# Second FFNs of a macaron block: g^T from turned experts and turned sums, instead of turning g

## The chip, the cores and the metric

The kernel runs on one core of a Trainium2 chip. Five engines work side by side: TensorE (PE, with its weight loads shown as PEld), VectorE (DVE), ScalarE (ACT), GpSimd (POOL) and SyncE (SP), which here issues every DMA. The metric is the device time of one execution in microseconds (us); the time before is the median of three runs.

## The reference, cut to what matters

The input x has shape (2, 2048, 1024), everything in float32. Three residual steps follow one another, each on a layer norm of x:

```python
x = x + 0.5 * ffn(layernorm(x), A, B, W, bias)      # "first FFN"
x = x + ssm(layernorm(x), ...)                      # state-space scan over time
x = x + 0.5 * ffn(layernorm(x), A, B, W, bias)      # "second FFN", the same weights

def ffn(x, A, B, W, bias):                          # a = 64 experts, r = 16
    vecs = einsum('arh,bsh->bsar', A, x)
    arrows = norm(vecs, axis=-1)
    routes = one_hot(top_k(arrows, 4)).sum(-2) / 4  # per row: 4 of 64 experts
    v = einsum('bsa,bsar->bsr', routes, vecs)       # 16 sums per row
    delta = einsum('bsa,ajr,bsr->bsj', routes, B, v)
    return einsum('bsh,jh->bsj', x, W) + bias + delta
```

Call g the array with `g[s, r, a] = routes[s, a] * v[s, r]`, 16 x 64 = 1024 columns for a row. Then `delta = g @ B`, a product over 1024, just as `x @ W` is.

## The kernel before

**Tiles.** The 4096 rows are cut into 16 chunks of 256 rows (8 per batch element), and a chunk into two blocks of 128 rows. `ffn(kind, c, i)` (L592) adds the work of one block of chunk c: kind "f" is the first FFN, "g" the second; 64 blocks in all. `prepare(c)` (L722) normalises a chunk's rows, turns them to u, projects them and computes the step sizes; `scans(c)` (L863) runs the scan of a chunk over 256 time steps.

**One FFN block.** Three products with [128 x 1024] operands: x with A (into the pair of PSUM banks `pv`), x with W and g with B (both accumulated into the pair `po`). Each is 16 float32 matmuls of 128x512; `products` (L575) issues them as tasks of four. A matmul needs its left operand turned, contraction on the partitions. x^T (`xnt`) comes from DRAM for kind "f" (the host laid it out); for kind "g" it is turned on PE: the scan's result y lies turned in DRAM, is fetched as `yt`, turned back on PE (`back`, L384), added to x1 by DVE (`summed`), and the sum is turned again (`turn`, L553). Between the A product and g stand: `square` (ACT, L631), `choose` (DVE, L641: norms, top 4, routes; its last step writes the routes into the tile `choice`), `routed` (DVE, L658), `total` (DVE, L668: the 16 sums, also into `choice`), `spread` (POOL, L676: g as a product of two broadcasts). Then `turn` makes g^T: eight 128x128 transposes on PE into two banks, two copies by ACT into `gt`. After the B products `close` (DVE, L694) scales and adds the result to x.

**Buffers.** Five PSUM banks serve everything of this kind. A block's `pv` and `po` pairs and the scan's sums are only taken if one bank stays free. There is one buffer each for `g`, `gt` and `yt`, two for `xnt`, `xg` and `choice`, four for `rep` (the scan's broadcast input), sixteen for `h`.

**Scan.** For each of four pairs of 128 channels of a chunk, sixteen units run ACT `decay` (two exponentials of 128x256), DVE `entry` (a product) and two DVE `scan` instructions, ACT `keep` (the state) and POOL `leave` (a product) and `join` (a sum). PE `total` (L973) then sums over states. SP fetches `rep` with a broadcast, two DMAs a unit pair.

**Order.** Nothing is left to a compiler: `Plan` (L77) collects tasks with an engine, a cost, the keys they read and write, the buffers they take and give, and a rank. `order()` (L126) plays them through: at each moment an idle engine takes the ready task of lowest rank whose buffers are free; a task becomes ready on another engine `HOP` after what it needs has ended, a DMA `land` after its issue. The resulting list is emitted as it is, so each engine's instructions stand in that fixed order, and so do SP's DMAs. Costs, landings and ranks are numbers in the code. The W and B products of a block have ranks near -1000, so that they go before nearly everything else on PE; the A products have the block's number n (0 to 63) in the sequence `f_seq`, where first FFNs run three chunks ahead of second ones.

**Start.** `load_all` (L408) loads the weights and takes their column means out of A and W (layer norm's mean): POOL sums the pieces of W (`gather`, L445), PE makes the means (`mean`, L472), DVE subtracts them (`center`, L481). Until then the first block's A product is corrected on PE (`correct`, L461).

Of the kernel before, what the change touches and what calls it, by code (L numbers as in the profile page):

```python
# [36 lines left out]
P = 128  # L37
# [3 lines left out]
TOPK = 4  # L41
# [35 lines left out]
class Plan:  # L77
# [3 lines left out]
    HOP = 0.14  # L81
# [145 lines left out]
def macaron_kernel(  # L227
# [55 lines left out]
    places("choice", 2, [P, NA + len(PADS) + RANK])  # L283
# [7 lines left out]

    plan.pool("x1_d", [dram.tile([P, D], FP, name=f"x1_d{j}") for j in range(2 * NT * 4)])
# [52 lines left out]
    def load_rows(c, i):  # L345
# [16 lines left out]
        if c == 0:  # L362
            add("SP", 0.4, load_t, [], [(xt, 0), (xt, 1)], rank=-74.6 * n - 1008.5 if n else -2000.0,
                take=[xt], land=2.3)
            add("SP", 0.4, load, [], row(x_p), rank=81.1 * n - 1006.8, take=[x_p], land=1.9)
        else:
            add("SP", 0.8, emit, [], [(x_p, q) for q in range(KC)] + [(xt, 0), (xt, 1)],
                rank=n - (1006.5 if c == 1 else 100.0), take=[x_p, xt], land=4.9)

    def load_sum(c, i, rank):  # L370
# [4 lines left out]
        for g in range(2):  # L375
# [8 lines left out]
            def back(g=g, pt=pt, yt=yt):  # L384
# [7 lines left out]
                [(yt, 0)] + ([] if g else row(x_p)), rank=200.9 + rank,  # L392
                take=[yt] if g else [x_p, yt], give=[y_d, x1_d], land=4.3)
# [5 lines left out]
            add("PE", 0.55, back, [(yt, 0)] + row(x_p, g), [(pt, 0)], rank=-38.4 + rank, take=[pt], give=[yt])  # L399
            add("DVE", 0.71, summed, [(pt, 0)] + row(x_p, g), row(x_p, g), rank=-60.6 + rank,  # L400
# [7 lines left out]
    def load_all():  # L408
        def one(dst, src, key, us, rank):
            keys = [(*key, h) for h in range(2)] if isinstance(key, tuple) else [key]  # L410
            add("SP", us, lambda: nc.sync.dma_start(out=dst, in_=src), [], keys, rank=rank, land=3.2)
# [11 lines left out]
        add("POOL", 0.23, lambda: nc.gpsimd.memset(mean_w.tile, 1.0 / D), [], [(mean_w, 0)],  # L423
# [15 lines left out]
        add("PE", 1.3, mean_x, [(xnt, 0), (xnt, 1), (mean_w, 0)], [(pm, 0)], rank=-1200.0, take=[pm],  # L439
            give=[mean_w])  # L440
        add("ACT", 0.36, minus, [(pm, 0)], [(less_m, 0)], rank=-1200.0, take=[less_m], give=[pm])
        for w_sb, name, key in ((wa, "wa", "pv"), (ww, "ww", "po")):
# [9 lines left out]
            for h in range(2 if name == "wa" else 0):  # L452
# [14 lines left out]
                add("PE", 0.47, correct, [(total, 0), (less_m, 0)], [(start[key][h], 0)], rank=-1400.0,  # L467
                    give=[total, less_m])
            for h in range(2):
# [8 lines left out]
                add("PE", 0.59, mean, [(total, 0), (mean_w, 0)], [(pt, 0)], rank=-1000.0, take=[pt],  # L478
                    give=[total, mean_w])
                for k in range(KC):  # L480
# [4 lines left out]
                    add("DVE", 0.55, center, [(pt, 0)], [(name, k, h)], rank=-900.0, give=[pt])  # L485
# [5 lines left out]
        add("POOL", 2.53, lambda: nc.gpsimd.tensor_scalar_mul(half_bias, half_bias, 0.5),  # L491
            [], ["half_bias"], rank=232.4)
# [7 lines left out]
        add("ACT", 0.31, exp_a, [], ["a_neg"], rank=87.5)  # L500
        add("DVE", 0.24, neg_a, [], ["a_neg"], rank=69.0)
# [6 lines left out]
    def spread_of(x_p, st, factor, rank, after=()):  # L508
# [28 lines left out]
        add("DVE", 1.95, stats, row(x_p) + list(after), [(st, 0)], rank=-70.5 + rank, take=[st])  # L537
        add("ACT", 2.63, root, [(st, 0)], [(st, 1)], rank=97.4 + rank)

    def normalize(x_p, xn_p, rank, after=()):  # L540
# [9 lines left out]
        add("ACT", 1.63, scale, row(x_p) + [(st, 1)], [(xn_p, 0), (xn_p, 1)], rank=-24.1 + rank,  # L550
            take=[xn_p], give=[st, x_p])

    def turn(src, keys, dst, out_keys, rank, take=(), give_src=None):  # L553

        for g in range(2):
# [9 lines left out]
            def act(g=g, pt=pt):  # L565
# [3 lines left out]
                rank=-40.0 + rank, take=[pt] + (list(take) if g == 0 else []),  # L569
                give=[src] if give_src else [])  # L570
            add("ACT", 0.58, act, [(pt, 0)], out_keys(g), rank=-141.8 + rank, give=[pt])
# [20 lines left out]
    def ffn(kind, c, i):  # L592
# [21 lines left out]
        for h in range(2):  # L614
# [4 lines left out]
            add("POOL", 1.19, bias, row(x_p, h) + ["half_bias"], row(x_p, h), rank=rank, port=True)  # L619
# [7 lines left out]
        for h in range(2):  # L627
# [10 lines left out]
            add("ACT", 1.02, square, [(pv[h], 0)], [(g_p, h)], rank=-67.7 + rank,  # L638
                take=[g_p] if h == 0 else [])

        def choose():  # L641
# [3 lines left out]
            routes = ch.tile[:, : NA + len(PADS)]  # L645
# [7 lines left out]
            nc.vector.tensor_scalar(routes, routes, CHOSEN, 1.0 / TOPK, ALU.is_equal, ALU.mult)  # L653

        add("DVE", 2.39, choose, [(g_p, 0), (g_p, 1)], [(ch, 0)], rank=-11.4 + rank,
            take=[ch, mk], give=[mk])
        for h in range(2):
# [7 lines left out]
            add("DVE", 0.62, routed, [(pv[h], 0), (ch, 0)], [(g_p, h)], rank=-234.6 + rank,  # L665
                give=[pv[h]])

        def total():  # L668
            nc.vector.tensor_reduce(  # L669
                ch.tile[:, NA + len(PADS) :],  # L670
                g_p.tile.rearrange("p (r a) -> p r a", a=na), AX.X, ALU.add,
            )

        add("DVE", 1.21, total, [(g_p, 0), (g_p, 1)], [(ch, 1)], rank=-13.0 + rank)
        for h in range(2):
            def spread(h=h):  # L676
                v0 = NA + len(PADS) + h * r2
                nc.gpsimd.tensor_mul(  # L678
                    g_p.tile[:, h * HD : (h + 1) * HD].rearrange("p (r a) -> p r a", a=na),
                    ch.tile[:, :NA].unsqueeze(1).to_broadcast([P, r2, NA]),  # L680
                    ch.tile[:, v0 : v0 + r2].unsqueeze(2).to_broadcast([P, r2, NA]),
                )

            add("POOL", 0.99, spread, [(ch, 0), (ch, 1)], [(g_p, h)], rank=-18.0 + rank, port=True,
                give=[ch])
        turn(g_p, lambda g: [(g_p, g)], lambda g: gt.tile[:, g * HC : (g + 1) * HC, :],
             lambda g: [(gt, g)], rank, take=[gt], give_src=True)
# [3 lines left out]
        for h in range(2):  # L691
            products(turn_of, po, h, gt, wb, "wb", False, True, lambda: turn_of.number - 1000.0, [], [gt])

            def close(h=h):  # L694
# [7 lines left out]
                rank=-140.5 + rank, give=[po[h], st])  # L702
# [377 lines left out]
```

## Time and profile before

| what | us |
|---|---|
| median of three runs | 3133.61 (3132.05 to 3138.01) |
| the profiled execution | 3132.46 |
| its span, first to last instruction | 3130.3 |
| PE busy | 3080.1 (98%) |
| DVE busy | 2811.7 (90%) |
| POOL busy | 2280.5 (73%) |
| ACT busy | 1866.3 (60%) |
| granted clock of TensorE, mean | 0.998 |

| group (line, what) | count | busy us | mean ns |
|---|---|---|---|
| L579 A, W and B products, 128x512 | 6144 | 907.4, 891.0, 894.1 | 593 to 595 |
| L561 transposes of g, 128x128 | 512 | 71.7 | 276 |
| L566 ACT copy to gt, 128x512 | 128 | 70.5 | 592 |
| L678 POOL spread, 128x512 | 128 | 139.2 | 1108 |
| L933 DVE scan, 128x256 | 2048 | 1407.7 | 731 |
| L918 ACT decay, 128x256 | 2048 | 974.0 | 478 |

A float32 matmul stands in the trace as two instructions, so 1024 matmuls of each FFN product appear as 2048. Matmuls overlap, so the mean of one is longer than the distance between two starts. A line of waits reads: engine, instruction that waited, "<-" what released it: total us, times, longest.

### The profile page before, as it was taken

What the parts mean: (1) busy time and instruction counts of PE and PEld (TensorE: products, weight loads), DVE (VectorE), ACT (ScalarE), POOL (GpSimd) and SP (SyncE); (2) the same over time, 40 slices, a digit from 0 to 9 for tenths busy, and PEclk for the clock granted to TensorE, in tenths of its full rate; (3) what the DMA queues carried; (4) which work ended last, traced back from release to release, by engine and by line L of the source; (5) the groups of instructions that cost most, each with busy time, mean ns of one, the idle gap of its engine ahead of it and who ended that gap; (6) DMA issues with size and microseconds to landing.
All of it is one profiled execution on the core that took longest, in us unless ns stands there. A gap on an engine that the chain in (4) does not pass through costs nothing.

```text
span 3130.3 us, 36399 instructions
## 1 busy us (share of the span) xinstructions
PE 3080.1 (98%) x9276; PEld 1433.7 (46%) x9276; DVE 2811.7 (90%) x4683; ACT 1866.3 (60%) x4851; POOL 2280.5 (73%) x1818
## 2 busy tenths in 40 slices
PE   7999999999999999999999999999999999999999
PEld 3444444444444444444444444444444444444444
DVE  5279999999999999999989999999999999999951
ACT  2266666666766666767666666666665655555531
POOL 3148787777788877787767777777888788888840
PEclk9999999999999999999999999999999999999999
DMA  6155644655455554554644655456454554555520
GB/s 231 54 162 153 188 142 140 192 153 174 153 164 164 161 177 149 163 173 144 181 148 135 190 153 169 148 156 183 141 171 142 161 162 138 155 161 149 149 73 15
DMA packets 306994, 478.69 MB, mean 153 GB/s; under 512 B 27360, under 2 KB 151904, under 8 KB 306784
## 3 DMA queue, kind: packets, MB, share of 16 engines
q1 hardware_dynamic: 306784, 476.36, 50.3%
q8 instruction: 74, 1.21, 0.2%
q14 instruction: 136, 1.11, 0.1%
HBM read 375.07 MB, written 101.19 MB: 152 GB/s over the span
## 4 chain that ended last, share of the span: by engine, by line
PE 60%; DVE 12%; issue 3%; ACT 2%; DMA 2%; POOL 1%; SPq 0%; DVEq 0%; POOLq 0%; ACTq 0%
PE bank L579 53%; DVE h L933 5%; PE bank L975 3%; DVE h L926 2%; PE bank L561 2%; PE bank L749 1%; PE bank L798 1%; PE bank L386 1%; ACT da L918 1%; DMA xf<-in_x 1%; DVE stats L513 1%; DVE g L659 1%; DVE norms L646 1%; DMA yt<-y_d 0%; DVE choice L653 0%
## 5 line engine op out<-in xcount | busy, mean ns | idle before, releaser
L946 POOL TENSOR_TENSOR h<-h,c 128x512 f32<-128x512 f32 x1024 | 1322.2, 1300 | 419.4 <-ACT state L943 397.9
L933 DVE TENSOR_TENSOR_SCAN h<-da,state,h 128x256 f32<-128x256 f32 x2048 | 1407.7, 731 | 14.1 <-ACT da L918 11.8
L918 ACT ACTIVATE da<-rep,a_neg 128x256 f32<-128x256 f32 x2048 | 974.0, 478 | 673.8 <-DVE h L933 637.2
L579 PE MATMUL bank<-wa,xnt 128*128 128x512 f32 x2048 | 907.4, 595 | 1.4 <-ACT xnt L566 1.4
L579 PE MATMUL bank<-wb,gt 128*128 128x512 f32 x2048 | 894.1, 594 | 6.3 <-ACT gt L566 6.2
L579 PE MATMUL bank<-ww,xnt 128*128 128x512 f32 x2048 | 891.0, 593 | 2.3 <-DVE ww L483 2.3
L965 POOL TENSOR_TENSOR h<-h,h 128x512 f32<-128x512 f32 x512 | 651.4, 1272 | 40.1
L926 DVE TENSOR_TENSOR h<-rep,b 128x512 f32<-128x512 f32 x1024 | 671.6, 665 | 1.4 <-ACT b L880 0.9
L579 PEld LDWEIGHTS bank<-ww,xnt 128*128 128x128 f32 x2048 | 389.7, 190 | 494.1 <-issue 482.7
L579 PEld LDWEIGHTS bank<-wb,gt 128*128 128x128 f32 x2048 | 384.1, 190 | 476.8 <-issue 455.5
L579 PEld LDWEIGHTS bank<-wa,xnt 128*128 128x128 f32 x2048 | 380.5, 190 | 454.1 <-issue 444.1
L678 POOL TENSOR_TENSOR g<-choice 128x512 f32<-128x512 f32 x128 | 139.2, 1108 | 228.7 <-DVE choice L669 228.6
L943 ACT COPY state<-h 128x2 f32<-128x2 f32 x1024 | 188.3, 185 | 55.4 <-DVE h L933 54.3
L632 ACT ACTIVATE g<-bank 128x512 f32<-128x512 f32 x128 | 133.8, 1046 | 74.5 <-PE bank L579 54.5
L533 ACT ACTIVATE stats<-stats 128x1 f32<-128x1 f32 x288 | 58.3, 202 | 139.4 <-DVE stats L528 133.2
L513 DVE BATCH_NORM_STATS2 stats<-xf 128x6 f32<-128x512 f32 x128 | 81.6, 678 | 60.4 <-DMA xf<-in_x 60.4
L617 POOL TENSOR_TENSOR xf<-xf,half_bias 128x512 f32<-128x512 f32 x64 | 83.8, 1329 | 59.3 <-DVE stats L513 59.2
L617 POOL TENSOR_TENSOR xg<-xg,half_bias 128x512 f32<-128x512 f32 x64 | 81.8, 1286 | 60.1 <-PE bank L561 36.9
L975 PE MATMUL bank<-h,summer 128*32 128x512 f32 x1024 | 123.1, 598 | 0.0
L646 DVE TENSOR_REDUCE norms<-g 128x64 f32<-128x1024 f32 x64 | 77.0, 1203 | 46.1 <-ACT g L632 42.8
L534 ACT ACTIVATE stats<-stats,pads 128x1 f32<-128x1 f32 x288 | 111.3, 387 | 9.7
L696 DVE SCALAR_TENSOR_TENSOR xg<-bank,stats,xg 128x512 f32<-128x512 f32 x64 | 47.4, 741 | 70.4 <-PE bank L579 69.9
(85 smaller groups left out, 1935.2 us busy)
## 6 DMA issues: line engine op xcount, KB each, us to landing
rep<-du_d SPq DMA_DIRECT2D x1024, 256.0 KB, 3.6
xnt<-in_x_t SPq DMA_DIRECT2D x32, 512.0 KB, 3.9
xf<-in_x SPq DMA_DIRECT2D x32, 512.0 KB, 5.2
x_d<-xf SPq DMA_DIRECT2D x32, 512.0 KB, 3.3
u_d<-u SPq DMA_DIRECT2D x32, 512.0 KB, 4.6
ysb<-u_d SPq DMA_DIRECT2D x64, 256.0 KB, 3.2
du_d<-delta SPq DMA_DIRECT2D x32, 512.0 KB, 3.4
du_d<-u SPq DMA_DIRECT2D x32, 512.0 KB, 3.8
```

The lines of the kernel that those rows point to most:

```text
L513: nc.vector.bn_stats(st.tile[:, 6 * s : 6 * s + 6], x_p.tile[:, s * HD : (s + 1) * HD])
L579: nc.tensor.matmul(ps[h].tile, lhsT=lhs.tile[:, k, :], rhs=w[:, k, h * HD : (h + 1) * HD], start=start and k == 0, stop=stop and k == KC - 1,)
L617: nc.gpsimd.tensor_add(x_p.tile[:, cols], x_p.tile[:, cols], half_bias[:, cols])
L632: nc.scalar.activation(g_p.tile.rearrange("p (a r) -> p r a", r=RANK)[:, h * r2 : (h + 1) * r2, :], vecs(pv, h), AF.Square,)
L678: nc.gpsimd.tensor_mul(g_p.tile[:, h * HD : (h + 1) * HD].rearrange("p (r a) -> p r a", a=na), ch.tile[:, :NA].unsqueeze(1).to_broadcast([ ...
L918: nc.scalar.activation(da.tile[:, k, :], r.tile[:, k, 0, :], AF.Exp, scale=a_neg[:, q + k, j, hi : hi + 1],)
L926: nc.vector.tensor_mul(h.tile, r.tile[:, :, 1, :], bs[hi].tile.unsqueeze(1).to_broadcast([P, 2, TC]),)
L933: nc.vector.tensor_tensor_scan(h.tile[:, k, :], da.tile[:, k, :], h.tile[:, k, :], state[:, q + k, j, hi : hi + 1], ALU.mult, ALU.add,)
L943: nc.scalar.copy(state[:, q : q + 2, j, hi : hi + 1], h.tile[:, :, TC - 1 : TC])
L946: nc.gpsimd.tensor_mul(h.tile, h.tile, cs[hi].tile.unsqueeze(1).to_broadcast([P, 2, TC]))
L965: nc.gpsimd.tensor_add(first.tile, first.tile, h.tile)
L975: nc.tensor.matmul(y.tile[j // 2 * 2 * DB : (j // 2 + 1) * 2 * DB, :], lhsT=summer[:, DB * (1 - j % 2) : DB * (3 - j % 2)], rhs=sums[j].ti ...
```

## The change

For the second FFN blocks (all of kind "g" but the very last one, 31 in number) g is no longer formed row by row and turned. Since g^T is, on its 1024 rows (r, a), the product of the turned routes (the same 64 rows for every r) and the turned sums (the same row for all 64 a), the two factors are turned and multiplied:

- `choose` writes the routes twice side by side (2 x 64 columns), with its marks kept in the tile `g` instead of `choice`; `choice` gets one buffer.
- `turn_s` on PE turns the 16 sums ([16 x 128]) and the doubled routes ([128 x 128]) into one bank.
- `take_s` and `take_c` on ACT copy both into `g`.
- `put_s` on SP writes the turned sums, 8 KB, to DRAM (`s_d`); `fetch_s` reads them back with two DMAs, each giving every one of 64 partitions the 8 rows of its half, so that `gt` holds 8 blocks of 128 columns.
- `spread` on POOL multiplies `gt` in place, in two halves, by the turned routes.

First FFN blocks keep the old way (`spread_t` and `turn`). The costs, landings and ranks of nearly all tasks and `HOP` are other numbers, so the order of every engine's instructions is another. One of them: the second block's x^T is loaded behind the pieces of A instead of before them.

```diff
-    HOP = 0.14
+    HOP = 0.11
...
-    places("choice", 2, [P, NA + len(PADS) + RANK])
+    places("choice", 1, [P, 2 * NA + RANK])
...
+    plan.pool("s_d", [dram.tile([RANK, P], FP, name=f"s_d{j}") for j in range(4)])
...
-            add("SP", 0.4, load_t, [], [(xt, 0), (xt, 1)], rank=-74.6 * n - 1008.5 if n else -2000.0,
-                take=[xt], land=2.3)
+            add("SP", 0.4, load_t, [], [(xt, 0), (xt, 1)], rank=0.8 * n - 1008.5 if n else -2000.0,
+                take=[xt], land=3.5)
...
-            add("PE", 0.55, back, [(yt, 0)] + row(x_p, g), [(pt, 0)], rank=-38.4 + rank, take=[pt], give=[yt])
+            add("PE", 0.55, back, [(yt, 0)] + row(x_p, g), [(pt, 0)], rank=-28.7 + rank, take=[pt], give=[yt])
...
-            routes = ch.tile[:, : NA + len(PADS)]
+            routes = g_p.tile[:, : NA + len(PADS)]
...
-            nc.vector.tensor_scalar(routes, routes, CHOSEN, 1.0 / TOPK, ALU.is_equal, ALU.mult)
-
-        add("DVE", 2.39, choose, [(g_p, 0), (g_p, 1)], [(ch, 0)], rank=-11.4 + rank,
+            nc.vector.tensor_scalar(
+                ch.tile[:, : 2 * NA].rearrange("p (s a) -> p s a", s=2),
+                routes[:, :NA].unsqueeze(1).to_broadcast([P, 2, NA]),
+                CHOSEN, 1.0 / TOPK, ALU.is_equal, ALU.mult,
+            )
+
+        add("DVE", 2.42, choose, [(g_p, 0), (g_p, 1)], [(g_p, 0), (ch, 0)], rank=-86.8 + rank,
             take=[ch, mk], give=[mk])
...
+        if kind == "f" or (c, i) == (NCH - 1, NT - 1):
+            for h in range(2):
+                def spread_t(h=h):
...
+            turn(g_p, lambda g: [(g_p, g)], lambda g: gt.tile[:, g * HC : (g + 1) * HC, :],
+                 lambda g: [(gt, g)], rank, take=[gt], give_src=True)
+        else:
+            pt, s_d = Place("bank"), Place("s_d")
+
+            def turn_s():
+                nc.tensor.transpose(pt.tile[:RANK, P : 2 * P], ch.tile[:, 2 * NA :], ident)
+                nc.tensor.transpose(pt.tile[:, :P], ch.tile[:, : 2 * NA], ident)
+
+            def take_s():
+                nc.scalar.copy(g_p.tile[:RANK, P : 2 * P], pt.tile[:RANK, P : 2 * P])
+
+            def take_c():
+                nc.scalar.copy(g_p.tile[:, :P], pt.tile[:, :P])
+
+            def put_s():
+                nc.sync.dma_start(out=s_d.tile, in_=g_p.tile[:RANK, P : 2 * P])
+
+            def fetch_s():
+                rows = s_d.tile.rearrange("(k s) t -> s k t", s=2)
+                for s in range(2):
+                    nc.sync.dma_start(
+                        out=gt.tile[s * NA : (s + 1) * NA, :, :],
+                        in_=rows[s].unsqueeze(0).to_broadcast([NA, KC, P]),
+                    )
+
+            add("PE", 0.31, turn_s, [(ch, 0), (ch, 1)], [(pt, 0), (pt, 1)], rank=-105.0 + rank, take=[pt], give=[ch])
+            add("ACT", 0.18, take_s, [(pt, 0)], [(g_p, 1)], rank=-138.5 + rank, give=[pt])
+            add("ACT", 0.34, take_c, [(pt, 1)], [(g_p, 0)], rank=-64.7 + rank, give=[pt])
+            add("SP", 0.4, put_s, [(g_p, 1)], [(s_d, 0)], rank=-33.4, take=[s_d], give=[g_p], land=3.0)
+            add("SP", 0.8, fetch_s, [(s_d, 0)], [(gt, 0), (gt, 1)], rank=-298.5, take=[gt], give=[s_d], land=4.6)
+            for h in range(2):
+                def spread(h=h):
+                    part = gt.tile[:, h * HC : (h + 1) * HC, :]
+                    nc.gpsimd.tensor_mul(
+                        part, part, g_p.tile[:, :P].unsqueeze(1).to_broadcast([P, HC, P])
+                    )
+
+                add("POOL", 1.1, spread, [(gt, h), (g_p, 0)], [(gt, h)], rank=-331.8 + rank, port=True, give=[g_p])
```

## The prediction

> **What bounds the kernel now.** I read the busy shares first, then the chain that ended last, then who waited for whom on TensorE, then the stretches of time.
>
> ```profile
> PE 3080.1 (98%) x9276; PEld 1433.7 (46%) x9276; DVE 2811.7 (90%) x4683; ACT 1866.3 (60%) x4851; POOL 2280.5 (73%) x1818
> ...
> PE 60%; DVE 12%; issue 3%; ACT 2%; DMA 2%; POOL 1%; SPq 0%; DVEq 0%; POOLq 0%; ACTq 0%
> ```
>
> TensorE (PE) is busy 98% and carries most of the chain. VectorE (DVE) is second, with the scans. The stretches (columns: window, length, busy PE, PEld, DVE, ACT, POOL) show where PE is not full:
>
> ```profile
> 20.00:40.00 20.00, 10.47 (x20) 3.83 (x18) 12.43 (x23) 4.87 (x12) 19.45 (x10) 0.78 1.02 377
> ...
> 600.00:1000.00 400.00, 394.53 (x1202) 184.85 (x1202) 388.73 (x650) 266.27 (x696) 315.05 (x249) 1.00 0.53 161
> ...
> 2600.00:2900.00 300.00, 299.32 (x904) 135.82 (x902) 288.42 (x484) 164.79 (x452) 250.06 (x203) 1.00 0.53 154
> ...
> 3000.00:3050.00 50.00, 46.55 (x140) 21.02 (x139) 17.84 (x32) 9.54 (x27) 15.45 (x13) 1.00 0.17 53
> ```
>
> PE loses about 10 us in 20 to 40 us, about 1.4 us per 100 in the middle, and under 1 us in the 300 us from 2600. So a microsecond of PE work is worth a microsecond, and so is a bubble. DVE, at 97% of these middle stretches, follows closely. The waits of PE name the holes:
>
> ```profile
> PE bank L473 <- POOL delta L448: 8.9, 1, 8.9
> PE bank L579 <- ACT gt L566: 6.2, 20, 1.3
> PE bank L386 <- DMA yt<-y_d: 5.8, 3, 3.4
> ...
> PE bank L579 <- DVE ww L483: 2.3, 1, 2.3
> ...
> PE bank L561 <- DVE xg L397: 1.9, 2, 1.1
> ```
>
> Two holes (8.9, 2.3) lie in the start; in the middle they are tenths of a microsecond. The last chain gives the spacing of PE's work (start, length, what):
>
> ```profile
> 2953.72 17.17 PE bank L579 x40
> 2970.89 1.31 PE bank L561 x12
> ...
> 2986.00 1.85 PE bank L975 x16
> ```
>
> A product pass costs 17.17/40 = 0.429 us (two passes per float32 product, so a half row block of eight products is 6.87), a transpose 1.31/12 = 0.109, a sums pass 0.116. I laid both PE instruction orders out end to end with these spacings: 3028.6 us of work before, 3008.4 after.
>
> **The change, part by part.**
>
> *Transposes.* 31 of the 64 row blocks lose eight transposes of g and get two (sums, experts): 31 x 6 x 0.109 = **-20.3 us**, all on PE. ACT trades two copies of 0.59 for two of an unseen 16- and 128-row size; between 128x2 (0.185) and 128x256 (0.37), I take 0.28. ACT is 60% busy, so only the one in the new chain counts. The Trainium skill (TensorE: Matmul & The Clock Gate, Part 4) gives about 275 ns for a transpose in a kernel; this trace's median duration is 273 ns too, but they overlap and start 0.109 apart. Priced by that duration the gain would be 51 us; I go by the spacing.
>
> *Start.* In the changed order 6.87 us of the second block's first product (x with A) stand ahead of the means that wait 8.9 us for POOL, and 3.43 more ahead of the product that waits 2.3 for DVE. Gain 6.87 + 2.3 = **-9** (bounds 0, if the waits merely move, and 11.2). Its x^T now loads behind A's eight pieces, whose products run from 8 to 23 us here; it is wanted at about 27.
>
> *The new round trip.* After a second-FFN block's W products, PE turns the sums (0.24 with its fill); ACT copies (0.28); SP puts 8 KB to DRAM; SP fetches 2 x 256 KB back in 512-byte rows; POOL multiplies the first half; only then may the B products start. No row shows these two transfers. Nearest:
>
> ```profile
> yt<-y_d SPq DMA_DIRECT2D x64, 256.0 KB, 4.8
> ...
> bc_d<-part SPq DMA_DIRECT2D x16, 32.0 KB, 2.9
> ```
>
> and, of POOL's products,
>
> ```profile
> L946 POOL TENSOR_TENSOR h<-h,c 128x512 f32<-128x512 f32 x1024 | 1322.2, 1300 | 419.4 <-ACT state L943 397.9
> ```
>
> The put is nearest bc_d<-part (landing 1.5 to 4.5, median 2.9); a fetch nearest yt<-y_d, same bytes and row length (3.0 to 8.4, median 4.8), and the second is issued 0.5 later. POOL's in-place product is nearest L946, 1.30 (g's own, 1.04, is the lower bound). With 0.05 per hand-over: 0.24 + 0.28 + 2.9 + 5.3 + 1.3 + 0.4 = **10.4 us**; with the shortest landings 7.2, with the longest 15.6. Cover is the PE work standing between the turn and the B products. In the changed order it is 11.4 to 12.3 in sixteen of the first twenty blocks (twelve transposes and three quarters of the next block's first product), so 1.0 to 1.9 are to spare, and 9.3 to 10.7 in four; the last eleven have 4.0, 6.3, 11.9, 8.4, 8.9, 6.8 and five times 8.9, to which the bubbles of the next paragraph add up to 1.9. Five blocks fall short, by 0.8 (the first, 9.3), 6.3, 2.6, 0.4 and 2.7: **+12.9**.
>
> The Trainium skill (DMA: Bandwidth & Descriptors, Latency and other measured facts) puts the fixed cost of a DMA at about 2 us, while its Rules for kernel authors call transfers under 64 KB mostly overhead, which speaks against an 8 KB put in PE's path. By 2 us in place of the row's 2.9 for the put, the five shortfalls would estimate to 9 and the lateness below to 4, and the sum to about no change. The sum here stays with the row.
>
> *Bubbles of the new order.* From 2490 us of PE work on only second-FFN blocks are left. There the order puts y's transposes, x1's transposes and the A products directly behind each other, after the W products: PE must wait for DVE's sum (0.68 + hand-overs = 0.79, as "PE bank L561 <- DVE xg L397" shows on a small scale) nine times, against two before: 7.1 - 1.6 = +5.5; for ACT's copy of xnt (0.59 + 0.10 = 0.69) twelve times, once 0.5: +8.8; for the second y fetch (4.8, cover 4.4) six times 0.4: +2.3; once 0.8 for the row scaled for the scan. Together **+17.4**. In the order before, these pairs have other products between them, and its PE waits there are nil. Half-hidden g copies (6.2 us over 20 waits) fall a little: **-1.3**.
>
> *Lateness.* The 26 blocks with cover enough still have four queues in their path: ACT's take stands behind decays (0.98 a pair), SP's put and fetch behind rep fetches and y_d puts, POOL's product behind leave and join (1.3). SP shows what a queued fetch may wait for:
>
> ```profile
> SPq L891 <- DVE h L926: 1060.8, 398, 11.8
> ...
> SPq L994 <- DVE ysb L988: 120.1, 54, 29.3
> ```
>
> PE now leans on the scan stream's timing. Against it: ACT's g copies, queued in the same way, cost hardly more than their own 0.24 each. Bounds 0 and 26 x 1.5 = 39 (half a decay, half a POOL product, half a microsecond of landing); near the lower, since the queues were on time: 0.3 x 26 = **+8**.
>
> *Costed at nothing.* DVE's choose writes 128 columns instead of 68: at most 0.342 (128x128) less 0.196 (least of L653), x 64 = 9 us, beside W products; it counts if DVE binds. POOL gains 62 x 0.26 = 16 us, at 73%. SP's fetch waits for its put's landing with rep fetches queued behind it; four rep buffers (16 us of scan work) cover 2.9. The other queue moves (one choice buffer, g held until the product) end 14 us or more before PE's next need; without that cover, 1 to 3 us a block.
>
> **Sum:** -20.3 - 9 + 12.9 + 17.4 - 1.3 + 8 = +7.7. The profiled execution took 3132.46 us (span 3130.3), so 3140.2; the median of the runs, 3133.61, lies 1.15 above it: **3141 us**, +0.24%. A measurement tells 0.2% (6.3 us) from no change.
>
> **Rivals.**
>
> *A. The round trip is quick: faster.* If put and fetch land near their shortest (1.5, 3.0), the chain is 7.2 to 8.5: the shortfalls shrink to about 4 and lateness to 0: -20.3 - 9 + 4 + 17.4 - 1.3 = -9, 3125; where late bubbles also vanish because PE would have waited for nothing else there (PE runs ahead), down to 3108. It decides once the chain is under about 9 us. For: the medians of such transfers include queueing. Against: 153 GB/s of scan traffic stays. Centre 3120.
>
> *B. The scan stream binds.* The order wants the last sums after 2886.8 us of PE work instead of 2926.4, with 121.6 us of PE work behind them instead of 102.2. DVE must finish about 20 us sooner. It idles some 105 us from 200 to 3000, half for PE, so it can; if it can't, 3016 (last sums now) - 9 + 122 + 20 of bubbles: 3149 to 3152.
>
> *C. The round trip is late in most blocks,* by 1.5 us beyond the sum's 0.3: 3141 + 31 = 3172; or by 1: 3162.
>
> *D. It does nothing:* gain and bubbles cancel, 3133.
>
> **How the numbers follow.** Forecast 0.45 (own range 3130 to 3152), A 0.28, B 0.12, C 0.10, D 0.05. A lies under 3127.3, with 0.03 of the forecast: faster 0.31. D and 0.14 of the forecast lie within: same 0.19. Slower 0.50. The range takes A down to 3112, B, and C to 3163, leaving out about 0.07 and 0.06.
>
> **What would show it.** PE instructions 186 fewer. The wait of PE's products for POOL (the gt product) totalling 13 to 25 us, the longest near 6 at about 2580 to 2620 us; of transposes for xg, 7; the hole at 26 us under 3. gt<-s_d landing near 5, s_d<-g near 3. Wrong if the fetch lands in 3.5 (A), if last sums come after 3010 (B), or if PE's wait for gt recurs in every block above 1 us (C).

## The result, and the profile after

The changed kernel takes 3183.22 us (median of four runs, 3177.49 to 3185.31) against 3132.83 for the kernel before on the same chip: a ratio of 1.0155, 95% interval 1.0137 to 1.0173. That is 50 us slower where 8 were forecast, and above the top of the range, 3163. The profiled execution has a span of 3180.4 us and a mean granted clock of 0.995 (before: 3130.3 and 0.998).

The busy shares and the chain that ended last, after:

```profile
PE 3081.2 (97%) x9090; PEld 1416.1 (45%) x9090; DVE 2816.8 (89%) x4683; ACT 1857.3 (58%) x4851; POOL 2282.7 (72%) x1818
...
PE 68%; DVE 15%; DMA 6%; issue 4%; ACT 3%; POOL 2%; SPq 1%; DVEq 0%; POOLq 0%; ACTq 0%
```

186 TensorE (PE) instructions are gone, as the change says, and yet PE's busy time is the same: 3081.2 against 3080.1. That is the first thing to explain; the second is the idle time, which grew from 50.2 to 99.2 us. Who made PE wait, after (us in total, times, longest):

```profile
PE bank L580 <- POOL gt L729: 25.1, 15, 5.1
PE bank L580 <- ACT xnt L567: 10.9, 18, 1.3
PE bank L562 <- DVE xg L398: 10.2, 9, 2.7
PE bank L387 <- DMA yt<-y_d: 6.4, 6, 2.2
PE bank L580 <- ACT gt L567: 5.8, 12, 1.6
PE bank L562 <- ACT delta L854: 5.3, 9, 1.7
...
PE bank L474 <- DVE g L664: 2.4, 1, 2.4
...
PE bank L474 <- POOL delta L449: 1.9, 1, 1.9
```

The first row is new: the B products waiting for POOL's product (the round trip). The next two have grown most: the wait for ScalarE's copy of xnt (1.4 before) and for VectorE's sum xg (1.9 before), the bubbles of the new order. The hole at the start shrank from 8.9 and 2.3 to 1.9 and 2.4. By stretches (window, length, busy PE, PEld, DVE, ACT, POOL, clock, DMA share, GB/s):

```profile
20.00:40.00 20.00, 15.65 (x35) 6.39 (x34) 14.31 (x25) 1.92 (x2) 17.49 (x8) 0.93 1.00 372
...
600.00:1000.00 400.00, 392.98 (x1173) 179.73 (x1172) 384.24 (x645) 257.51 (x682) 310.05 (x244) 1.00 0.56 165
...
2600.00:2900.00 300.00, 277.58 (x784) 122.92 (x785) 282.95 (x460) 165.19 (x447) 239.40 (x191) 0.98 0.57 159
```

The late stretch, where PE was full before (299.32 of 300), loses 22 us, and its clock is 0.98. The timeline of PE in it shows one block from its turn to its B products, and two later runs of B products (start, length, what, idle time before it):

```profile
2617.20 0.27 PE L701 MATMUL bank<-ident,choice 128*16 128x128 f32 x1
2617.31 0.27 PE L702 MATMUL bank<-ident,choice 128*128 128x128 f32 x1
...
2620.64 1.93 PE L1021 MATMUL bank<-h,summer 128*32 128x512 f32 x16 [0.78 <-ACT state L989]
2627.63 15.70 PE L580 MATMUL bank<-wb,gt 128*128 128x512 f32 x32 [5.07 <-POOL gt L729]
...
2683.21 14.00 PE L580 MATMUL bank<-wb,gt 128*128 128x512 f32 x32 [1.91 <-POOL gt L729]
...
2739.69 13.90 PE L580 MATMUL bank<-wb,gt 128*128 128x512 f32 x32
```

From the turn of the sums to the B products it takes 2627.63 - 2617.20 = 10.4 us, and 5 of them are uncovered. Then the 32 instructions of the B products take 15.70, where 32 of them undisturbed take 13.90 (at 2739.69) and 32 behind a stop of 1.91 us take 14.00 (at 2683.21). The windows right behind the stop say why:

```profile
2626.00:2628.00 2.00, 0.37 (x1) 0.30 (x2) 2.00 (x5) 1.58 (x4) 1.69 (x2) 0.99 1.06 256
2628.00:2630.00 2.00, 2.00 (x3) 0.67 (x2) 2.00 (x5) 1.27 (x4) 2.00 (x3) 0.50 0.90 242
2630.00:2632.00 2.00, 2.00 (x4) 0.86 (x3) 2.00 (x4) 1.19 (x4) 2.00 (x3) 0.65 0.66 218
2632.00:2634.00 2.00, 2.00 (x6) 0.95 (x5) 2.00 (x4) 1.19 (x4) 1.92 (x3) 1.00 0.47 137
```

PE is called busy all through 2628 to 2632, but at a clock of 0.50 and 0.65 it gets 7 instructions done where the next 2 us alone hold 6. So a stop has a price after its end, which the listed wait doesn't contain and which the busy time hides.

### The profile page after: what moved, and what is told of

The parts are those of the page before. It is cut to its first block, busy times and chain, and to the rows that moved or that the text cites. A ratio compares the mean times of both kernels' runs of the same rounds, so it can differ in the third digit from the quotient of the medians.

```text
span 3180.4 us, 36244 instructions
## 1 busy us (share of the span) xinstructions
PE 3081.2 (97%) x9090; PEld 1416.1 (45%) x9090; DVE 2816.8 (89%) x4683; ACT 1857.3 (58%) x4851; POOL 2282.7 (72%) x1818
## 4 chain that ended last, share of the span: by engine, by line
PE 68%; DVE 15%; DMA 6%; issue 4%; ACT 3%; POOL 2%; SPq 1%; DVEq 0%; POOLq 0%; ACTq 0%
PE bank L580 61%; DVE h L979 6%; DVE h L972 3%; PE bank L1021 3%; DMA gt<-s_d 2%; PE bank L562 1%; DMA xf<-in_x 1%; PE bank L795 1%; DMA s_d<-g 1%; ACT da L964 1%; DVE g L664 1%; POOL h L992 1%; PE bank L844 1%; DVE norms L647 1%; DVE stats L514 1%
## 5 line engine op out<-in xcount | busy, mean ns | idle before, releaser
L580 PE MATMUL bank<-wb,gt 128*128 128x512 f32 x2048 | 900.8, 598 | 31.1 <-POOL gt L729 25.1
L580 PE MATMUL bank<-wa,xnt 128*128 128x512 f32 x2048 | 915.4, 598 | 12.2 <-ACT xnt L567 10.9
L685 POOL TENSOR_TENSOR g<-choice 128x512 f32<-128x512 f32 x66 | 69.3, 1071 | 166.0 <-DVE choice L674 143.8
L729 POOL TENSOR_TENSOR gt<-gt,g 128x512 f32<-128x512 f32 x62 | 77.5, 1272 | 107.0 <-DMA gt<-s_d 107.0
```

Source lines behind the costliest of these rows:

```text
L580: nc.tensor.matmul(ps[h].tile, lhsT=lhs.tile[:, k, :], rhs=w[:, k, h * HD : (h + 1) * HD], start=start and k == 0, stop=stop and k == KC - 1,)
```

## The experiments

Each was timed beside the kernel before on the same chip; that kernel's median was 3134 to 3137 us in these groups. Where nothing else is said, the edit is made to the changed kernel.

### The same order, with a fetch that doesn't wait for the put

```diff
-                rows = s_d.tile.rearrange("(k s) t -> s k t", s=2)
+                rows = x[0, :2, :].rearrange("a (k t) -> (a k) t", t=P).rearrange("(k s) t -> s k t", s=2)
```

> The changed kernel with every engine's order untouched; only the fetch reads 2048 floats of the input x instead of the sums just put, so it no longer waits for the put to land (the sums never reach g^T: that part of the computation is left out). Theory 1 (PE's stops at the round trip, each with its restart and, after the longest, a stretch of half clock, are the main loss): the put's landing of 3.2 us leaves a chain of about 10.4, PE's wait for the gt product falls from 25.1 to under 8 us, and the time from 3183 to 3150-3165. Theory 2 (the scan stream binds, PE's stops are only where its slack shows): the stops move elsewhere, 3178-3188. Theory 3 (the new numbers of the order are bad, whatever the path): hardly any change, 3175-3188.

Measured: 3178.58 us, ratio 1.0134 (1.0112 to 1.0157). The fetch no longer waits for the put, yet only 5 us come back, which the two intervals don't tell from nothing; Theory 1's 3150 to 3165 is missed. The wait for POOL is still 23.4 us in 11 places. This edit doesn't price the whole transfer: the fetch stays, and it landed later after its issue, in 5.3 us in the median (3.6 to 9.1) where the changed kernel's took 4.3 (3.5 to 6.4). POOL's timeline for the block shown above (here the turn begins at 2612.4, and the fetch is issued 1.1 us later instead of 4.0):

```profile
2617.41 1.27 POOL L1011 TENSOR_TENSOR h<-h,h 128x512 f32<-128x512 f32 x1
2618.63 2.49 POOL L992 TENSOR_TENSOR h<-h,c 128x512 f32<-128x512 f32 x2
2621.08 2.49 POOL L729 TENSOR_TENSOR gt<-gt,g 128x512 f32<-128x512 f32 x2
```

In this block POOL has no idle time ahead of the product: it stands in POOL's list behind `leave` and `join` of the scan. In the changed kernel it waited for the transfer there only 0.32 us:

```profile
2623.49 2.49 POOL L992 TENSOR_TENSOR h<-h,c 128x512 f32<-128x512 f32 x2
2626.31 2.50 POOL L729 TENSOR_TENSOR gt<-gt,g 128x512 f32<-128x512 f32 x2 [0.32 <-DMA gt<-s_d]
```

So here the transfer and POOL's queue end nearly together, and taking one away shows the other. That is so in three of the 11 places; in the other eight POOL stood idle until the fetch had landed, for 0.2 to 6.2 us. An earlier fetch was worth little in this order; a quicker one was not tried.

### The new numbers with the old way of g

```diff
-        if kind == "f" or (c, i) == (NCH - 1, NT - 1):
+        if True:
```

> The changed kernel with all 64 blocks on the old way (g formed and turned), all costs, landings and ranks new; the order is played through again. Theory 1: no round trip, the start's gain stays: 3122-3145. Theory 2: PE has 20 us more work than in the changed kernel and the scan stream is unchanged: 3180-3195. Theory 3: the bubbles of the order stay: 3165-3190.

Measured: 3153.88 us, ratio 1.0056 (1.0039 to 1.0072). That lies between the ranges of the three theories. The new costs and ranks alone cost some 18 us, faster start included; the rest, about 30 us, comes with the round trip in this order.

### The new way of g with the old numbers

The kernel before with the new tasks added, `HOP` and all old costs and ranks kept:

```diff
-        turn(g_p, lambda g: [(g_p, g)], lambda g: gt.tile[:, g * HC : (g + 1) * HC, :],
-             lambda g: [(gt, g)], rank, take=[gt], give_src=True)
+        if kind == "f" or (c, i) == (NCH - 1, NT - 1):
...
+        else:
...
+            add("PE", 0.31, turn_s, [(ch, 0), (ch, 1)], [(pt, 0), (pt, 1)], rank=-105.0 + rank, take=[pt], give=[ch])
```

> The kernel before with the new way in the 31 blocks, but its own costs, landings and ranks for all old tasks (the new tasks have the changed kernel's). Theory 1: the stops come with the path: 3155-3200, PE's waits for the gt product above 15 us. Theory 3: with the old numbers the path gives its gain: 3110-3125. Theory 2: near the kernel before, 3130-3140.

Measured: 3299.05 us, ratio 1.0519 (1.0499 to 1.0538), 99 us above the highest range. The longest of PE's waits:

```profile
PE bank L580 <- POOL gt L728: 97.2, 20, 11.4
```

The new numbers are no ornament: in the old order 20 blocks wait for POOL's product, up to 11.4 us each, and the mean clock falls to 0.977.

### Only the last three chunks the old way

```diff
-        if kind == "f" or (c, i) == (NCH - 1, NT - 1):
+        if kind == "f" or c >= NCH - 3:
```

> The changed kernel with the old way kept also in the second FFN blocks of the last three chunks, where few other products are left to cover the round trip; new way in 26 blocks. Theory 1: late stops go (about 17 us of waits, their restarts and slow clock), 4 us of transposes come back: 3145-3165. Theory 2: 3175-3190. Theory 3: 3170-3190.

Measured: 3174.03 us, ratio 1.0128 (1.0104 to 1.0153), inside Theory 3's range and just under Theory 2's. From 2600 to 2900 us PE is busy 275.76 of 300, no better than 277.58: the long stops belong to chunks 10 to 12, which this edit leaves as they are. It tells little but that.

### The B products without g^T

```diff
-                        lhsT=lhs.tile[:, k, :],
+                        lhsT=(lhs.tile if fixed is None else fixed)[:, k, :],
...
+            products(turn_of, po, h, gt, wb, "wb", False, True, lambda: turn_of.number - 1000.0, [], [gt], fixed=None if kind == "f" or (c, i) == (NCH - 1, NT - 1) else ww[:, :, :P])
```

> The changed kernel in its own order on every engine, but the B products of the 31 blocks of the new way take a fixed operand (a part of W) and so wait for nothing of the round trip, which still runs beside them (g^T does not enter the result of these blocks). Theory 1 (PE's stops at the round trip cost their wait, a restart, and after the long ones slow clock): 25 us of waits, 15 restarts of 0.2 and some 5 us of clock go: 3145-3160. Theory 2 (the scan stream and POOL's queue bind; PE's stops only show slack): the stops come back at other places, 3170-3185.

Measured: 3162.65 us, ratio 1.0082 (1.0065 to 1.0099). The wait for POOL is gone, and with it 21 of the 50 us, a little less than Theory 1 expected. (The profiled execution was the slowest of four, 3170.9.) The longest waits that remain are the bubbles, unchanged:

```profile
PE bank L562 <- DVE xg L398: 10.9, 9, 2.8
PE bank L580 <- ACT xnt L567: 10.9, 18, 1.3
```

### The old way from chunk 10 on

```diff
+        if kind == "f" or c >= 10:
```

> The changed kernel with the old way kept from chunk 10 on (12 blocks instead of 1), the new way in 20 blocks; order played through anew. Late stops between 2600 and 2900 us (22 us idle in the changed kernel, none in the kernel of old path and new numbers) should go. Theory 1: 3183 - 22 - 10 (restarts, clock) + 7 (transposes) = 3150-3162. Theory 2: no better than with the old way from chunk 13, 3170-3180. If the round trip pays at all where it has cover, this must lie under the kernel of old path and new numbers, 3154.

Measured: 3156.21 us, ratio 1.007 (1.0055 to 1.0085), and PE is busy 296.68 of 300 from 2600 to 2900 again. It is the old way that helps in the late chunks; but the result is not below that of the old way in all chunks (3153.88). The twenty blocks where cover was enough on paper bring nothing either: the wait for POOL is still 11.8 us in ten of them.

### The kernel before, with the changed place of one load

```diff
-            add("SP", 0.4, load_t, [], [(xt, 0), (xt, 1)], rank=-74.6 * n - 1008.5 if n else -2000.0,
+            add("SP", 0.4, load_t, [], [(xt, 0), (xt, 1)], rank=0.8 * n - 1008.5 if n else -2000.0,
```

> The kernel before with one rank changed: the second block's x^T is loaded behind the pieces of A, as in the changed kernel, so that its first product can fill the wait for the means. If the start's gain (wait of 8.9 us for POOL down to 2 to 4) is real and nothing later gives it back: 3124-3130. If the later order only has longer to wait elsewhere: 3131-3137.

Measured: 3130.86 us (ten runs), ratio 0.9983 (0.9974 to 0.9992), faster than both kernels, if by less than 0.2%; it lies between the two ranges. The hole at the start is 7.3 us instead of 8.9. Of the forecast's start gain this one load carries a small part; the other ranks of the start were not tried by themselves.

### Short stops, put into the kernel before

To price a stop by itself, a copy of two columns of a left operand onto themselves is put on ScalarE at the border of two tasks of one product, so that PE's next matmul waits for it:

```diff
+    def stop(part):
+        for _ in range(1):
+            nc.scalar.copy(part, part)
```

> The kernel before, in its own order, with 55 short stops of TensorE between 600 and 2700 us: at the border of two tasks of the same product ScalarE copies two columns of the left operand onto themselves, so that TensorE's next matmul waits for ScalarE. Nothing is left out. From ScalarE's rows (0.19 to 0.39 us for an instruction of this size, and up to 0.48 of a decay that is just running) one stop waits some 0.6 us, 33 us in all. Theory 1 (a stop costs its wait and about 0.25 us of restart; short ones don't lower the clock): the span grows by 33 + 14 = 47 us, a third more than the waits that the profile shows, to about 3180, and the granted clock stays at 0.997 or more. Theory 2 (a stop costs its wait and nothing else): the span grows by the waits alone, 33 us, to about 3167.

Measured: 3173.48 us, ratio 1.0128 (1.0113 to 1.0143), so 40 us more. The busy shares and the wait:

```profile
PE 3097.6 (98%) x9276; PEld 1429.9 (45%) x9276; DVE 2808.2 (89%) x4683; ACT 1874.6 (59%) x4906; POOL 2283.3 (72%) x1818
...
PE bank L581 <- ACT xnt L1038: 25.3, 55, 2.1
```

The waits were shorter than expected, 25.3 us and most of them 0.28. The excess is as Theory 1 has it: 40 against 25, and PE's busy time rose by 17.5 us (3097.6 - 3080.1) with the same 9276 instructions. Summing (1 - clock) over windows of 4 us gives 10.3 us lost to a lower clock, against 6.8 before; the mean is 0.996, where Theory 1 said 0.997 or more. The other 14.0 us, over 55 stops, are 0.25 us a stop beside its wait, the figure of Theory 1. Two rows show what it is made of. A matmul of a product is on record for 0.595 us, but the next one starts 0.429 after it; where the next has to wait, this overlap of 0.17 is lost. And the 32 B products behind a stop at full clock took 14.00 us instead of 13.90, another 0.10.

### Long stops, put into the kernel before

```diff
+        for _ in range(12):
```

> The same, with 11 stops in place of 55, of twelve copies each, so that one waits about 3 us, 33 us in all, as much as the short ones. Theory 1 (a stop of more than about 2 us is followed by a stretch at a lower granted clock, which costs 1.5 to 2 us each, beside 0.25 of restart): the granted clock falls to about 0.992, the span grows by 33 + 3 + 11 x 1.75 = 55 us, to about 3188, and windows of 2 us right behind each stop show a clock near 0.5. Theory 2 (waits alone): the span grows by 33, to 3167, with the clock as before, 0.998.

Measured: 3178.03 us, ratio 1.0143 (1.0128 to 1.0159), 45 us more, 10 less than Theory 1's sum and 12 more than Theory 2's. The busy shares, and the wait:

```profile
PE 3095.7 (97%) x9276; PEld 1437.1 (45%) x9276; DVE 2810.7 (89%) x4683; ACT 1891.4 (60%) x4983; POOL 2282.1 (72%) x1818
...
PE bank L581 <- ACT xnt L1038: 35.5, 11, 4.6
```

Busy time rose by 15.6 us, 1.4 for each of the 11 stops, and the mean clock fell to 0.993: the same sum over windows gives 20.5 us, 13.7 more than before. What is left of the busy time, 1.9 us, is 0.17 a stop. The stop that ended at 779.22 (2.78 us), the windows around it, and one laid on the slow stretch:

```profile
778.00:780.00 2.00, 0.78 (x2) 0.49 (x3) 2.00 (x3) 1.01 (x6) 0.00 (x0) 1.00 0.16 36
780.00:782.00 2.00, 2.00 (x4) 0.86 (x3) 1.97 (x3) 0.00 (x0) 0.00 (x0) 0.61 0.49 163
782.00:784.00 2.00, 2.00 (x3) 0.67 (x2) 2.00 (x4) 0.17 (x1) 1.36 (x2) 0.54 1.00 343
784.00:786.00 2.00, 2.00 (x6) 0.95 (x5) 2.00 (x4) 1.19 (x4) 1.67 (x2) 1.00 0.06 18
...
780.40:783.80 3.40, 3.40 (x5) 1.35 (x4) 3.40 (x5) 0.00 (x0) 1.16 (x2) 0.51 0.82 278
```

Some 3.4 us at half clock, then full speed: 1.7 us lost. Nine of the eleven stops (2.78 to 4.61 us) are followed by such a stretch; those at 979.42 (2.78) and 2440.81 (3.15) are not. Of the five longest among the short stops, those of 1.24, 1.71, 1.87 and 2.11 us are followed by full clock, one of 2.01 by 0.51 and 0.64. So the price of a stop of this length is a chance, not a constant: 1.7 us where it falls due. (Nine times that is 15.4; the sum above has 13.7 since the first 100 us lost 5.1 in this run and 6.8 before.)

### The late turns first

```diff
-            add("PE", 0.55, back, [(yt, 0)] + row(x_p, g), [(pt, 0)], rank=-28.7 + rank, take=[pt], give=[yt])
+            add("PE", 0.55, back, [(yt, 0)] + row(x_p, g), [(pt, 0)], rank=-28.7 + rank + (-1500.0 if c >= 10 else 0.0), take=[pt], give=[yt])
...
-                 lambda g: [(xnt, g)], rank, take=[xnt])
+                 lambda g: [(xnt, g)], rank, take=[xnt], up=-1500.0 if c >= 10 else 0.0)
```

> The changed kernel with one more edit: for chunks 10 to 15 TensorE's turns of y and of x1 get a rank 1500 lower, so that they go ahead of the products that would otherwise stand before them, and the sums and copies that they wait for are covered by those products. Nothing is left out. Theory 1 (the bubbles of the new order are a loss of their own beside the round trip, priced at 17.4 us in the prediction, 21 as the waits for xg and xnt were measured): these waits fall by 10 or more and the time by about as much, to 3165 to 3175. Theory 2 (the late part is bound by something behind these waits, the scan's sums or the round trip): the waits move to other rows and the time stays at 3178 to 3188.

Measured: 3159.1 us, ratio 1.008 (1.0064 to 1.0097): 24 us less than the changed kernel, more than Theory 1 expected. (Its profiled execution was the slowest of four, 3169.1, 13 us less than the changed kernel's; the others lie between 3156.6 and 3159.9.) The waits:

```profile
PE bank L580 <- POOL gt L729: 15.8, 12, 3.2
PE bank L580 <- ACT xnt L567: 6.1, 11, 1.8
...
PE bank L1021 <- POOL h L1011: 5.3, 2, 2.7
PE bank L562 <- DVE xg L398: 3.6, 3, 1.4
```

The waits for xg and xnt fell by 11.4, and the one for POOL by 9.3 too, since the moved turns now cover the round trip: in the last eleven blocks it fell from 12.1 to 2.9. A new row has come: PE's sums wait for the scan's `join` at the end of the scan.

### Both repairs, and the old way with the late turns first

The edit just shown, first together with the one that takes g^T out of the B products:

```diff
+                        lhsT=(lhs.tile if fixed is None else fixed)[:, k, :],
...
+                 lambda g: [(xnt, g)], rank, take=[xnt], up=-1500.0 if c >= 10 else 0.0)
```

> Two edits on the changed kernel together: the B products of the 31 blocks take a slice of W as left operand, so that they wait for no g^T (this leaves the second FFNs' g out of the result; all else is done), and the late turns of y and x1 go first, as in late_turns_first. Alone they gave 21 us (3162.65) and 24 us (3159.1). Theory 1 (two separate kinds of stops, round trip and bubbles, make up nearly all of the loss): the gains add, 3183 - 45 = 3138, between 3132 and 3146. Theory 2 (they are stops of the same late stretch, and taking away one kind lets the other, or VectorE's scans, come forward): the sum is well short of that, 3150 to 3160.

Measured: 3161.59 us, ratio 1.0077 (1.006 to 1.0093). The gains of 21 and 24 don't add: both edits together are worth what each is alone. Theory 2 was right, and the profile shows what comes forward. In the last stretch of the scan (late turns first, then both edits):

```profile
3000.00:3050.00 50.00, 47.11 (x134) 19.80 (x132) 48.87 (x82) 26.87 (x78) 43.85 (x36) 1.00 0.37 108
```

```profile
2900.00:3000.00 100.00, 98.84 (x283) 44.65 (x282) 97.73 (x167) 56.00 (x159) 86.55 (x70) 1.00 0.56 169
...
PE bank L387 <- DMA yt<-y_d: 12.1, 7, 4.2
PE bank L562 <- DVE xg L398: 8.1, 4, 4.0
PE bank L1021 <- POOL h L1011: 7.3, 4, 2.8
```

VectorE is full in these stretches, and PE waits for what the scan delivers. The last sums begin at 3043.1 us (before: 3016.3, the changed kernel: 3047.8). The old way with the new numbers has them at 3045.3, so the scan ends late without any round trip too. With both edits the scan is on time for long: 1792 of its 2048 scan instructions have begun by 2682.4 us, against 2685.9 before. It falls behind after that (before, the old way with the new numbers, both edits):

```profile
2800.00:2900.00 100.00, 99.85 (x303) 44.92 (x302) 96.02 (x161) 52.75 (x143) 84.28 (x69) 1.00 0.56 161
2800.00:2900.00 100.00, 99.85 (x313) 47.58 (x312) 82.29 (x130) 59.27 (x143) 59.62 (x48) 1.00 0.46 140
2800.00:2900.00 100.00, 97.98 (x298) 45.93 (x297) 83.68 (x128) 57.85 (x142) 59.56 (x47) 1.00 0.48 140
```

VectorE is idle for 16 to 18 of these 100 us, where it was idle for 4, while PE is full or nearly so with other work. Which of the new numbers starves the scan there was not tried.

Then together with the old way of g in all blocks:

```diff
+        if True:
...
+                 lambda g: [(xnt, g)], rank, take=[xnt], up=-1500.0 if c >= 10 else 0.0)
```

> The changed kernel's numbers with the old way of g in all blocks, as in old_path_new_numbers (3153.88), and the late turns of y and x1 first, as in late_turns_first (3159.1 with the round trip). Nothing is left out. Theory 1 (the late bubbles come with the round trip's order; with the old way TensorE was 299.61 of 300 us busy from 2600 to 2900 already): nothing changes, 3148 to 3158, and the round trip, with its bubbles repaired, still costs about 5 us in spite of the 20 us of transposes it saves. Theory 2 (the new numbers carry the bubbles whatever the path): the gain is the same as with the round trip, 3130 to 3138.

Measured: 3154.81 us, ratio 1.0062 (1.004 to 1.0084), as expected by Theory 1: the edit does nothing with the old way. Against 3159.1 with the round trip the intervals overlap. So with its bubbles repaired, the round trip is worth between nothing and a small loss, although it takes 20 us of work from PE.

## Why the prediction was wrong

The direction was right, at a chance of 0.50. The size was wrong by 42.4 us (50.1 measured on the two spans, 7.7 forecast), and the two traces divide it by where PE's time went: PE's idle time grew by 49.0 where the sum had 28.0 of stops (-9 + 12.9 + 17.4 - 1.3 + 8), and busy time grew by 1.1 where the sum had -20.3.

**The step that failed: a stop was priced at its wait.** 42.4 = 21.0 of more idle time + 21.4 inside PE's busy time. For the second part the prediction has no term at all. All rows of PE's waits together count 100 stops after and 57 before; 43 more at the measured 0.25 are 11 us. The lower clock, summed over windows, costs 17.0 us after and 6.8 before, 10 more. Together 21. Both prices are shown by the inserted stops, on the kernel before and without any round trip. The profile of before showed them hardly at all: its clock was low only in the first 100 us (0.93), and a stop of 3.4 us at 378 was followed by full clock. The stretches of low clock after stand behind the stops of 3.05 us at 384, 2.74 at 1533, 2.17 at 1832, 5.07 at 2628 and 3.41 at 2883, and behind two short ones in a row, 0.97 and 0.68 at 2927 to 2928. A hint lay in the prediction's own numbers: the spacings laid end to end give 3028.6 us before, where the trace has PE busy for 3080.1, and the 51.5 us between them were passed over.

The Trainium skill (TensorE: Matmul & The Clock Gate, Part 1, What's actually happening) says that the clock drops to half after at least one idle window of about 3.4 us, and that the window runs freely. The half clock agrees. The length doesn't: here stops of 2.01 to 2.78 us brought it, and the pair that adds up to 1.65, while one of 3.15 did not. A stop of 1.36 us, before 442.2 us with the late turns first and before 443.5 in the changed kernel, was followed by half clock in the one (0.50 from 444 to 446) and by full clock in the other.

**A second step that failed: that the scan can end sooner.** The same 50.1 us can be divided at the last sums. They begin 31.5 us later than before (3047.8 against 3016.3), and 18.6 us more lie behind them (132.6 against 114.0). The second part is as forecast, 121.6 - 102.2 = 19.4. The first is not: the prediction wanted the scan to end about 20 us sooner and set the doubt aside with "It idles some 105 us from 200 to 3000, half for PE, so it can". The run of the old way with the new numbers shows the last sums 29.0 us late with no round trip, so this lies in the new order. And since they are still 26.8 us late with both kinds of stops repaired, repairing both brought back only about half of the 50 us.

**Transposes, -20.3.** The count was right, and nothing in the runs speaks against the price: the changed kernel is busy 7.8 us less than with the old way and the same numbers (3081.2 against 3089.0), with 31 more stops (100 against 69, 8 us at 0.25) and 5 us more of low clock (17.0 against 12.0) in it, so about -21 underneath.

**Start, -9.** The two waits fell from 11.2 to 4.3: -6.9. Near, and the hole was under 3 as said.

**The round trip, +12.9 and +8.** The wait for POOL came to 25.1, at the top of the 13 to 25 given, against 20.9 in the sum; the longest is 5.1, in the block at 2617 us that was named. In the last eleven blocks the term held nearly block by block: waits of 5.1, 1.9, 0.6, 0.7, 3.4 and 0.4, together 12.1, where 6.3, 2.6, 0.4, 0, 2.7 and 0 were said, together 12.0. In the first twenty, held to be covered but for one, nine waited, 13.1 together, against 0.8 and what the 8 us of lateness has for them. The mis-sized step there is the put, taken at 2.9. Its median, 3.2, is near, but it landed in 1.3 to 6.2, and in eight of these nine blocks in 4.7 to 6.2. One of them (turn at 1176.8):

```profile
1176.97 0.35 SPq L353 DMA_DIRECT2D xnt<-in_x_t  x1
1177.38 0.42 SPq L354 DMA_DIRECT2D xf<-in_x  x1
1177.90 0.38 SPq L711 DMA_DIRECT2D s_d<-g  x1
...
1183.80 1.28 SPq L716 DMA_DIRECT2D gt<-s_d  x2
...
1190.19 2.49 POOL L729 TENSOR_TENSOR gt<-gt,g 128x512 f32<-128x512 f32 x2 [2.81 <-DMA gt<-s_d]
...
1191.51 0.70 PE L580 MATMUL bank<-wb,gt 128*128 128x512 f32 x1 [2.21 <-POOL gt L729]
```

The put was issued behind two loads of 512 KB and landed 5.8 us later; the fetch followed at once. The other blocks show the same: of all 31 puts, 23 landed 0.17 to 0.58 us after the last transfer that SP had issued ahead of them, and the eight others in 1.34 to 1.37. The prediction asked how long such a transfer takes, and not what stands ahead of it. The fetch was as taken, 4.3 (5 said). In the late blocks that waited, SP issued the fetch 1.0 to 1.7 us after the put had landed in five of six, and POOL's product began without idle time, straight behind other work, in two. In all, the chain from the turn to POOL's first half came to 11.8 us in the median (8.2 to 15.3), where 10.4 was said. The Trainium skill's 2 us for the fixed cost of a DMA (DMA: Bandwidth & Descriptors, Latency and other measured facts) would have been too short for the put in 21 of the 31 blocks. "Near the lower, since the queues were on time" was an argument about other tasks.

**Bubbles, +17.4.** The waits for xg and xnt rose by 8.3 and 9.5, 17.8 against 14.3 for these two. One wait is as long as said (0.78 and 0.68, most of them), but the total is near by luck: from 2560 us on, where the term has them, they rose by 10.9 (14.2 against 3.3), and 6.9 us lie in earlier blocks that had no term. As a cost of their own they were sized too low: the late turns first gave back 24 us for 11 us of these waits, because the wait for POOL fell by 9.3 as well.

**What had no term.** Some 13 us more of idle time lie in small waits; about 2 of them, for y's fetch and for the scaled row, were in the sum. The largest are for delta, 5.3 (1.6 before), u, 3.5 (1.1 before), and the decays, 2.3 (none before). Those for u and the decays are there with the old way and the new numbers too (3.1 and 1.8), the one for delta is not (1.6). That run, without any round trip, is 18 us slower than the kernel before. The prediction had charged the new order only with its late bubbles, and of these it has next to none (0.8 for xg, 0.9 for xnt from 2570 to 3060).

**Rivals.** A (a quick round trip, 3120) falls: put and fetch landed in 3.2 and 4.3 us in the median, where A needed 1.5 and 3.0 (of yt<-y_d the shortest is in fact 2.7). B (the scan stream binds, from last sums after 3010 us) is half right. The last sums were late, 3047.8, but in the changed kernel PE's own stops held them back as well: without the wait for POOL they begin at 3036.5. With the stops repaired or the old way kept, the kernels lie at 3154 to 3162, near the 3149 to 3152 of B. C (late in most blocks) named the place: 15 of 31 blocks waited; its price of 1 to 1.5 us a block was of the right size for the waits, 25.1 / 15 = 1.7, but in half the blocks.

**Most likely cause.** Shown: the round trip's stops (21 us when removed), the late bubbles (24 when removed), the new numbers by themselves (18), and that these overlap, since the scan stream stands behind them. Not settled: which of the new costs and ranks leaves VectorE without scan work between 2800 and 2900 us.

## What to carry to other kernels

On an engine that is 98% busy, price a new wait at its length plus what it costs to start again (0.25 us here), and one of about 2 us or more at the chance of a slower clock behind it too (1.7 us here, and now and then behind shorter ones); windows of a low clock behind stops show it. When a path is moved through other queues, its length is set by the place of each step in those queues and not by the sum of durations; ask for each step what stands ahead of it in the order, and for a DMA which transfers were issued ahead of it. And when a change brings a new order, run the new order with the old path first: here it carried more than a third of the loss.

## What the runs showed of the hardware that was not expected

A stop of PE by 0.28 us costs about 0.5, and the other half appears as busy time. Behind 9 of 11 inserted stops of 2.78 to 4.61 us, the granted clock stood at 0.5 for some 3.4 us, so that a run of 24 matmul instructions took 12.26 us (at 779.22) instead of the 10.57 behind another stop of 2.78 us (at 979.42). PE's busy time can therefore stay the same (3081.2 against 3080.1) while 186 instructions leave it. A put of 8 KB landed in 1.34 to 1.37 us where the transfers issued ahead of it had landed by about then, and otherwise 0.17 to 0.58 us after the last of them, up to 6.2 us after its own issue.
